# Reordering one-term matrix products against longer steps in two gated layers, and loading the first blocks in halves

## The chip, the cores and the metric

The kernel runs on one core of a Trainium2 chip, in float32. The metric is the device time of one execution in microseconds (us). A profile of one execution gives, for each engine, the instructions with their start and length.

## What is computed

The input x has 512 channels and 64 x 64 pixels. Four layers each add their result to x; each begins with a group normalization over 32 groups of 16 channels.

```python
x = x + attention(gn(x))         # layer 0: 8 heads, 4096 tokens, softmax over negative squared distances
x = x + gated_conv(gn(x), L1)    # layer 1
x = x + gated_conv(gn(x), L2)    # layer 2
x = x + linear_attention(gn(x))  # layer 3, with a 5 x 5 depthwise convolution

def gated_conv(x):               # both gated layers
    fused = conv1x1(x, w_in) + b_in          # 512 -> 1024 channels
    pwa, abc = fused[:128], fused[128:]
    dw0, dw1, dw2 = split(dwconv7(abc))      # 128, 256, 512 channels
    h = pwa * dw0
    h = (conv1x1(h, pw0) + pw0_b) * dw1
    h = (conv1x1(h, pw1) + pw1_b) * dw2
    return conv1x1(h, w_out) + b_out
```

## The kernel before

x stays on the chip as X: four chunks of 128 channels, each in eight blocks of 512 pixels. TensorE (PE) multiplies into PSUM banks of 128 x 512; VectorE (DVE) or ScalarE (ACT) evicts them. `matmul` (L1147) fixes TensorE's order to the order in which the Python code issues the steps; the order on DVE and ACT comes from the tile framework's scheduler, apart from instructions that are pinned.

**The beginning.** `load_x` (L171 to L174) issues X's chunks 0 and 1 block by block, chunk 0 on the SP queue and chunk 1 on the ACT queue; chunks 2 and 3 follow on SP (`load_later`). Each queue keeps at most four transfers in flight: a fifth is issued when the first has landed. `measure` (L623) computes the statistics of one block on DVE; `first` lists the 16 blocks of chunks 0 and 1, `rest` the 16 of chunks 2 and 3. `parameters` (L631) drives `_Norm.params`, a chain of small steps: aggregate, a small matmul, squares, a second matmul, `gn_a` (L136), a square root on ACT (L137), reciprocal (L139) and correction, `gains` (L638). At each of its two yields and once after the square root it calls a function `meanwhile`; here each call measures one block of `rest`. The gains scale the first weights (L426, L432), and the first matmul (`begin`) follows.

**The gated layers.** `_gated_convs` runs for L1 and L2. Three kinds of steps are written into lists:

- `inputs(i)`, called b12, b34 and b56: the first 1x1 convolution by a Strassen-like method of seven products (`_Seven.steps`), in groups of seven steps p1, p5, p7, p2, p6, p3, p4 for two chunks and two blocks. Each step multiplies two terms. p1, p5 and p7 open banks `ps[0]`, `ps[1]` and `ps[2]`; p2, p3 and p4 add their product to these same banks, and `put` then evicts them (ACT L1181 after p2, DVE L1188 and L1191 later). After p1 and p5 ACT copies the bank (`keep`, L1416); after p7 DVE adds the bank into `kept[1]` (L537).
- `blocks(gate, i)`, called g[i]: one step per block. A product of the earlier h with a pointwise weight, then one DVE instruction that adds the bias and multiplies by the convolved plane (L1489). g[1] and g[2] have one term, g[3] and later two.
- `outputs(3)`, `outputs(4)`: one-term products with the output weight, evicted by DVE into X (L1508, L1512).

These products share a pool of four PSUM banks (`ps_mm`); the convolution has four of its own (`ps_cv`).

`convolve(i, first, between)` runs the depthwise convolution of chunk i: first the steps of the list `first`, then bursts of 48 small matmuls (`ps_cv`, some 1.5 us each), with steps of `between` spread over the gaps; each step carries a weight (0.5 for a step of seven, 0.25 per term of the others) by which it is spread. After the last burst come the DVE transposes of the result (L1280, then four of 128 x 1024 at L1286), each followed by a bias on ACT (L1602), while the rest of `between` runs. g[i] needs the finished chunk i. During a convolution ACT also makes shifted copies (S, L1226) for the next one.

So around the end of `convolve(2)` TensorE's order is: last burst, g1[2..7], p1 and p5 of b56, g2[0..7], p7 and p2 of b56, first burst of `convolve(3)`. At the end of `convolve(5)` it is: last burst, out, out, out, then two gate products of two terms, first burst of `convolve(6)`.

Of the kernel before, what the change touches and what calls it, by code (L numbers as in the profile page):

```python
# [16 lines left out]
P = 128  # L17
# [4 lines left out]
BLK = 512  # L22
NB = N // BLK
# [123 lines left out]
def _all(pieces):  # L147
    for _ in pieces:
        pass
# [12 lines left out]
@with_exitstack  # L162
def trunk_kernel(ctx: ExitStack, tc: tile.TileContext, a: dict, out: bass.AP):
    nc = tc.nc

    base = ctx.enter_context(tc.tile_pool(name="base", bufs=1))
    small = ctx.enter_context(tc.tile_pool(name="small", bufs=1))


    X = base.tile([P, NC, N], FP, tag="X", name="X")  # L170
    def load_x(chunks, engines):  # L171
        for b in range(NB):
            for c, eng in zip(chunks, engines):
                eng.dma_start(out=X[:, c, ts(b, BLK)], in_=a["x"][c, :, ts(b, BLK)])  # L174

    load_x((0, 1), (nc.sync, nc.scalar))

    vec = base.tile([P, NVEC], FP, tag="vec", name="vec")

    def load_later():  # L180
        load_x((2, 3), (nc.sync, nc.sync))
        nc.sync.dma_start(out=vec, in_=a["vecs"])

    def vcol(name, i):
        at, n = _VEC_AT[name]
        return vec[:, at + i : at + i + 1]

    def vall(name):
        at, n = _VEC_AT[name]
        return vec[:, at : at + n]  # L190

    ident = base.tile([P, P], FP, tag="ident", name="ident")
    make_identity(nc, ident)

    gmask = base.tile([P, P], FP, tag="gmask", name="gmask")
    nc.gpsimd.memset(gmask, 1.0 / GROUP)
    for cm, step, first in ((1, -GROUP, 0), (-1, GROUP, GROUP - 1)):
        nc.gpsimd.affine_select(
            out=gmask,
            in_=gmask,  # L200
            compare_op=ALU.is_ge,
            fill=0.0,
            base=first,
            pattern=[[step, P // GROUP], [0, GROUP]],
            channel_multiplier=cm,
        )

    neg2 = base.tile([D, 1], FP, tag="neg2", name="neg2")
    nc.vector.memset(neg2, -2.0)

    def new_stats():
        return small.tile([P, NC, NB, 6], FP, tag="stats", name="stats")

    centered = _Centered(tc, small)

    dram = ctx.enter_context(tc.tile_pool(name="dram", bufs=1, space=bass.MemoryType.DRAM))
    F = [dram.tile([P, FORM.planes, FORM.plane], FP, tag=f"F{i}", name=f"F{i}") for i in range(NDW)]
    F3 = [
        dram.tile([P, FORM3.planes, FORM3.plane], FP, tag=f"G{i}", name=f"G{i}")
        for i in range(NQKV)  # L220
    ]
    Z = dram.tile([NB, BLK], FP, tag="Z", name="Z")
    R = dram.tile([32, 32], FP, tag="R", name="R")

    def others(stats, norm, *hint):

        stats, norm = _gated_convs(
            tc, a, X, vcol, vall, gmask, small, new_stats, centered, stats, norm, F
        )
        _linear_attention(  # L230
            tc, a, X, vcol, vall, ident, gmask, small, centered, stats, norm, F3, Z, out, *hint
        )

    def past():

        for eng in nc.engines:
            done = [i for i in nc.cur_bb.bb.instructions if i.engine == eng]
            with tc.issue_after(done[-1]):
                tc.mark_branch_hint_location("general", "LikelyTaken", engines=[eng])

    okay = small.tile([1, 1], mybir.dt.int32, tag="okay", name="okay")
    stats = new_stats()
    opool = tc.alloc_tile_pool(name="opool", bufs=1, side="right")
    O = [opool.tile([P, N], FP, tag=f"O{i}", name=f"O{i}") for i in range(NC)]
    norm = _attention_pairs(tc, a, X, O, gmask, small, centered, stats, okay, load_later, R)
    opool.release()
    others(stats, norm, past)

    found = nc.values_load(okay[0:1, 0:1])
    with tc.If(found < 1, label="general"):  # L250
        stats = new_stats()
        _attention(tc, a, X, ident, gmask, neg2, small, centered, stats)
        norm = _Norm(nc, small, gmask)
        centered.by(norm)
        with tc.tile_pool(name="ps_n", bufs=2, space=PSUM) as ps_n:
            _all(
                norm.params(0, NC - 1, stats, lambda: ps_n.tile([P, BLK], FP, tag="mm", name="gn_ps"))
            )
        for k in range(2):
            for c in range(NC - 1):  # L260
                centered.take(_pixels(FORM, X[:, c, :], k), c)
        others(stats, norm)
# [310 lines left out]
def _attention_pairs(tc, a, X, QO, gmask, small, centered, stats, okay, load_rest, R):  # L573
# [12 lines left out]
    nc = tc.nc  # L586
# [6 lines left out]
    with tc.tile_pool(name="att0", bufs=1) as p0, tc.tile_pool(  # L593
# [22 lines left out]
        def taken(b, c0, c1, engines=(None,)):  # L616
            for c in range(c0, c1):
                tc.keep_in_program_order(
                    centered.take(X[:, c, ts(b, BLK)], c, engines[c % len(engines)])
                )  # L620

        def measure(b, c):
            tc.keep_in_program_order(nc.vector.bn_stats(stats[:, c, b, :], X[:, c, ts(b, BLK)]))  # L623

        first = [(b, c) for b in range(NB) for c in range(2)]
        rest = [(b, 2 + c) for b, c in first]
# [5 lines left out]
        def parameters(c0, c1, meanwhile, known):  # L632

            norm.pause = meanwhile
            for _ in norm.params(c0, c1, stats, bank_gn, known):
                meanwhile()
            for n, g in enumerate((2 * scale * gain_in, gain_in)):
                nc.vector.tensor_scalar(gains[:, n, c0:c1], norm.r[:, c0:c1], g, None, ALU.mult)  # L638
# [10 lines left out]
        def scaled_first(n, eng, c0=0, c1=NC, pinned=False):  # L649
            centered.scaled(w_first[n], gains[:, n // 2 if n > 1 else n], eng, c0, c1, pinned)  # L650
# [5 lines left out]
            load_w(n, nc.sync)  # L656
        for at in first:
            measure(*at)
        parameters(
            0, 2, lambda: measure(*rest.pop(0)), lambda: taken(0, 0, 2, (None, nc.gpsimd))  # L660
        )
        scaled_first(2, nc.scalar, 0, 2, True)
        scaled_first(0, nc.gpsimd, 0, 2)
        for k in range(1, NB // 2):
# [657 lines left out]
def _gated_convs(ctx, tc, a, X, vcol, vall, gmask, small, new_stats, centered, stats, norm, F):  # L1322
# [4 lines left out]
    nc = tc.nc  # L1327
# [13 lines left out]
    for layer in ("L1", "L2"):  # L1341
# [28 lines left out]
        def taken(k, chunks=range(NC), eng=None):  # L1370
            for c in chunks:
                ins = centered.take(pc.pixels(X[:, c, :], k), c, eng)
                if pinned:
                    tc.keep_in_program_order(ins)
# [211 lines left out]
        def outputs(*chunks):  # L1586
            n = len(chunks) / 4
            return [
                (n, lambda b=b, o=o: output(chunks, b, o))
                for b in range(NB // 2, NB)  # L1590
                for o in range(NC if b == NB // 2 else NC - 1)
            ]
# [3 lines left out]
        def convolve(i, first, between):  # L1596


            D[i] = hp.tile([P, N], FP, tag="h", name=f"h{i}")

            def bias(t):
                nc.scalar.activation(t, t, AF.Identity, bias=vcol(pre + "dw_b", i))  # L1602

            taps = a[f"{layer}_T"]
            later = [] if i < 2 else None
            pc.ahead(i, 0, taps, later=later)
            for n, (_, f) in enumerate(first):
                f()
                if later and n == 3:
                    for _ in range(4):  # L1610
                        tc.keep_in_program_order(nc.scalar.copy(*later.pop(0)))
            for pair in later or ():
                nc.scalar.copy(*pair)

            parts = FORM.nr // FORM.run
            total = sum(n for n, _ in between)
            late = total / 12
            done = 0
            for part, _ in enumerate(pc.conv(i, 0, taps, bias, D[i], True)):
                upto = total - late * min(parts + 2 - part, 3)  # L1620
                if part < parts:
                    upto = upto * (part + 1) / parts
                while between and done + between[0][0] / 2 <= upto + 1e-6:
                    n, f = between.pop(0)
                    f()
                    done += n
            for _, f in between:
                f()

        b12, b34, b56 = (inputs(i) for i in (2, 4, 6))  # L1630
        g = [blocks(gate, i) for i in range(NDW)]
# [24 lines left out]
                f()  # L1656
        convolve(0, b12[:10], b12[10:])
        convolve(1, b34[:6], g[0] + b34[6:20])
        convolve(2, [], b34[20:] + g[1] + b56[:2])
        convolve(3, g[2] + b56[2:4], b56[4:16])  # L1660
        convolve(4, [], b56[16:] + g[3][:2])
        convolve(5, [(0, load_out)] + g[3][2:6], g[3][6:] + outputs(3) + g[4][:2])
        rest = outputs(4)
        convolve(6, [], g[4][2:] + rest[:9])

# [896 lines left out]
```

## Time and profile before

| | us |
|---|---|
| median of 3 runs (lowest, highest) | 3707.27 (3705.42, 3708.36) |
| the profiled execution | 3706.54 |
| its span | 3704.8 |
| first statistic on DVE starts | 4.62 |
| first matmul on X starts | 20.60 |
| L1: last burst of `convolve(2)` to first of `convolve(3)` | 2377.68 to 2400.84 |
| L2: the same | 2848.14 to 2871.61 |

The profile page lists busy time by engine, the chain of work that ended last, and the costliest groups of instructions. A weight load (PEld) goes ahead of each matmul record; a float32 product of 128 x 512 and one term makes two such records. In the timeline the bracket behind a row is the idle time before it and the instruction that ended it.

### The profile page before, as it was taken

What the parts mean: (1) busy time and instruction counts of PE and PEld (TensorE: products, weight loads), DVE (VectorE), ACT (ScalarE), POOL (GpSimd) and SP (SyncE); (2) the same over time, 40 slices, a digit from 0 to 9 for tenths busy, and PEclk for the clock granted to TensorE, in tenths of its full rate; (3) what the DMA queues carried; (4) which work ended last, traced back from release to release, by engine and by line L of the source; (5) the groups of instructions that cost most, each with busy time, mean ns of one, the idle gap of its engine ahead of it and who ended that gap; (6) DMA issues with size and microseconds to landing.
All of it is one profiled execution on the core that took longest, in us unless ns stands there. A gap on an engine that the chain in (4) does not pass through costs nothing.

```text
span 3704.8 us, 81755 instructions
## 1 busy us (share of the span) xinstructions
PE 3666.8 (99%) x35068; PEld 1695.2 (46%) x35068; DVE 2728.9 (74%) x3577; ACT 2061.9 (56%) x3007; POOL 228.8 (6%) x221
## 2 busy tenths in 40 slices
PE   7999999999999999999999999999999999999999
PEld 6544444444465443444433344554445544445543
DVE  6677777777765777877878868766778667776647
ACT  3577774777744777747575555673347632355210
POOL 1000000000000000010000000001100002232212
PEclk9999999999999999999999999999999999999999
DMA  2000000000000000000000015782157721575322
GB/s 103 10 7 7 4 7 12 4 7 7 7 4 10 7 4 7 7 12 4 4 7 4 7 53 169 199 222 63 34 154 202 214 73 51 159 195 125 84 59 95
DMA packets 186035, 222.77 MB, mean 60 GB/s; under 512 B 15800, under 2 KB 128696, under 8 KB 185536
## 3 DMA queue, kind: packets, MB, share of 16 engines
q1 hardware_dynamic: 160672, 156.26, 15.7%
q10 hardware_dynamic: 21312, 48.03, 3.6%
q0 software_dynamic: 3680, 13.18, 1.1%
q8 instruction: 277, 4.54, 0.5%
q14 instruction: 94, 0.77, 0.1%
HBM read 157.51 MB, written 59.90 MB: 59 GB/s over the span
## 4 chain that ended last, share of the span: by engine, by line
PE 92%; DVE 3%; DMA 2%; issue 1%; POOL 1%; ACT 0%; SPq 0%; ACTq 0%; DVEq 0%; POOLq 0%
PE ps L1147 25%; PE av L865 24%; PE ps_s L847 24%; PE ps L495 5%; PE ps_cv L1147 5%; PE vkp L1147 3%; PE ps L563 3%; PE ps_o L495 2%; PE ps_t L2058 1%; PE ps_o L926 1%; DMA S<-G 1%; DVE h L1286 0%; DVE h L1489 0%; POOL X L1569 0%; PE ps_M L1147 0%
## 5 line engine op out<-in xcount | busy, mean ns | idle before, releaser
L855 ACT ACTIVATE pt<-ps_s,A 128x512 f32<-128x512 f32 x2048 | 1284.3, 685 | 448.8 <-PE ps_s L847 438.6
L847 PE MATMUL ps_s<-O,K 64*64 64x512 f32 x8192 | 1417.4, 589 | 0.0
L1024 DVE TENSOR_TENSOR acc<-acc,pt 128x1024 f32<-128x1024 f32 x960 | 1177.1, 1226 | 325.1 <-ACT pt L855 298.8
L865 PE MATMUL av<-pt,O 64*64 64x512 f32 x4096 | 745.2, 589 | 0.0
L865 PE MATMUL av<-pt,V 64*64 64x512 f32 x4096 | 673.7, 589 | 0.0
L847 PEld LDWEIGHTS ps_s<-O,K 64*64 64x64 f32 x8192 | 436.3, 133 | 518.2 <-issue 468.1
L1226 ACT COPY S<-S 32x1295 f32<-32x1295 f32 (+1 forms) x256 | 321.3, 1256 | 158.7 <-DMA S<-F 70.2
L865 PEld LDWEIGHTS av<-pt,O 64*64 64x64 f32 x4096 | 236.3, 133 | 254.0 <-issue 241.3
L865 PEld LDWEIGHTS av<-pt,V 64*64 64x64 f32 x4096 | 209.4, 133 | 268.2 <-issue 253.8
L1147 PE MATMUL ps<-diff,w_sum 128*128 128x512 f32 x516 | 242.4, 600 | 1.4 <-DVE plane L1191 1.0
L1147 PEld LDWEIGHTS ps_cv<-S,T 64*32 64x32 f32 x13824 | 192.7, 105 | 110.8 <-issue 71.1
L1147 PE MATMUL ps_cv<-S,T 64*32 64x128 f32 x13824 | 232.7, 272 | 4.2 <-issue 3.0
L491 DVE TENSOR_TENSOR diff<-X,diff 128x512 f32<-128x512 f32 x200 | 134.4, 683 | 31.3 <-PE ps L1147 31.0
L491 DVE TENSOR_TENSOR diff<-X 128x512 f32<-128x512 f32 x200 | 132.2, 683 | 26.2 <-PE ps L495 14.2
L1147 PE MATMUL ps<-h,pw_L 128*128 128x512 f32 x320 | 147.9, 602 | 3.0 <-DVE h L1489 2.1
L1147 PE MATMUL ps<-h,w_out_L 128*128 128x512 f32 x320 | 147.8, 600 | 1.7 <-DVE X L1512 1.7
L1147 PEld LDWEIGHTS ps<-diff,w_sum 128*128 128x128 f32 x516 | 94.6, 190 | 117.9 <-issue 105.7
L1147 PE MATMUL ps<-X,w_in_L 128*128 128x512 f32 x304 | 143.9, 602 | 1.0 <-ACT w_in_L L426 0.8
L1280 DVE STREAM_TRANSPOSE h<-ps_cv 128x512 f32<-128x512 f32 x112 | 109.6, 1052 | 39.9 <-PE ps_cv L1147 39.5
L1147 PE MATMUL vkp<-kT,vT 128*128 128x512 f32 x256 | 115.2, 592 | 0.0
L537 DVE TENSOR_TENSOR kept<-kept,ps 128x512 f32<-128x512 f32 x73 | 49.9, 683 | 79.3 <-PE ps L495 28.2
L419 ACT ACTIVATE X<-X,gn_less 128x512 f32<-128x512 f32 x113 | 71.5, 709 | 52.6 <-DVE gn_less L129 52.6
(302 smaller groups left out, 3532.5 us busy)
## 6 DMA issues: line engine op xcount, KB each, us to landing
T<-in_L_T_dram SPq DMA_DIRECT2D x112, 384.0 KB, 4.5
F<-plane ACTq DMA_DIRECT2D x112, 324.0 KB, 3.7
S<-F SPq DMA_DIRECT2D x224, 162.0 KB, 4.8
S<-G SPq DMA_DIRECT2D x96, 153.0 KB, 4.3
row<-G SPq DMA_DIRECT2D x48, 272.0 KB, 3.6
T<-in_L_T_dram SPq DMA_DIRECT2D x48, 256.0 KB, 4.1
G<-plane POOLq DMA_DIRECT2D x33, 289.0 KB, 3.1
rd<-R SPq DMA_DIRECT2D x64, 128.0 KB, 2.9
```

Source lines behind the costliest of these rows:

```text
L419: return self.nc.scalar.activation(xs, xs, AF.Identity, bias=less)
L491: yield eng.tensor_tensor(t[j][c], a(c), b(c), ALU.subtract)
L495: self.matmul(ps, w[:, c], hs[c], start=(first and c == 0), stop=(c == 1), skip_group_check=not first,)
L537: nc.vector.tensor_add(kept[1], kept[1], ps[2])
L563: self.matmul(ps[:, ts(i, P)], hs[c][:, ts(i, P)], w[:, c], start=(first and i == c == 0), stop=(c == 1), skip_group_check=True,)
L847: nc.tensor.matmul(ps[ts(half, D), ts(h, BLK)], K[rows, t * P + half * D : t * P + (half + 1) * D], QO[pair][rows, cols], start=True, stop ...
L855: nc.scalar.activation(pt[:, ts(h, BLK)], ps[:, ts(h, BLK)], AF.Exp, bias=A[:, t, h : h + 1])
L865: nc.tensor.matmul(av[half][rows, :], v[keys, t * P + h * D : t * P + (h + 1) * D], pt[keys, ts(h, BLK)], start=(t == 0), stop=(t == NT - 1),)
L1024: nc.vector.tensor_add(acc, acc if u > 1 else first, pt)
L1147: self.tc.keep_in_program_order(self.nc.tensor.matmul(*args, **kw))
L1226: nc.scalar.copy(second, first)
L1280: nc.vector.transpose(out, src)
```

## The change

Three edits: the first block of chunks 0 and 1 is loaded as two halves of 64 partitions, one on each queue; of the three blocks of `rest` measured inside `parameters(0, 2, ...)` the third, after the square root, is measured later; and in `_gated_convs` the same steps are put into another order in the lists for `convolve(2)`, `convolve(3)` and `convolve(5)`.

```diff
+    def load_x(chunks, engines, b0=0):
+        for b in range(b0, NB):
...
-    load_x((0, 1), (nc.sync, nc.scalar))
+    for c in range(2):
+        for half, eng in enumerate((nc.sync, nc.scalar)):
+            rows = ts(half, P // 2)
+            eng.dma_start(out=X[rows, c, 0:BLK], in_=a["x"][c, rows, 0:BLK])
+    load_x((0, 1), (nc.sync, nc.scalar), 1)
...
-        parameters(
-            0, 2, lambda: measure(*rest.pop(0)), lambda: taken(0, 0, 2, (None, nc.gpsimd))
-        )
+        spare = [lambda: measure(*rest.pop(0))] * 2 + [lambda: None]
+        parameters(0, 2, lambda: spare.pop(0)(), lambda: taken(0, 0, 2, (None, nc.gpsimd)))
...
-        convolve(2, [], b34[20:] + g[1] + b56[:2])
-        convolve(3, g[2] + b56[2:4], b56[4:16])
+        mixed = g[1][:5] + b56[:1] + g[1][5:7] + b56[1:2] + g[1][7:]
+        convolve(2, [], b34[20:] + mixed)
+        convolve(3, g[2][:2] + b56[2:3] + g[2][2:5] + b56[3:4] + g[2][5:], b56[4:16])
         convolve(4, [], b56[16:] + g[3][:2])
-        convolve(5, [(0, load_out)] + g[3][2:6], g[3][6:] + outputs(3) + g[4][:2])
+        o3 = outputs(3)
+        mixed = g[3][6:7] + o3[:7] + g[3][7:] + o3[7:9] + g[4][:1] + o3[9:11] + g[4][1:2] + o3[11:]
+        convolve(5, [(0, load_out)] + g[3][2:6], mixed)
```

## The prediction

> **What bounds the kernel now.** I read the page first: the busy line and the chain that ended last.
>
> ```profile
> PE 3666.8 (99%) x35068; PEld 1695.2 (46%) x35068; DVE 2728.9 (74%) x3577; ACT 2061.9 (56%) x3007; POOL 228.8 (6%) x221
> PE 92%; DVE 3%; DMA 2%; issue 1%; POOL 1%; ACT 0%; SPq 0%; ACTq 0%; DVEq 0%; POOLq 0%
> ```
>
> TensorE is the bound nearly everywhere, so an edit pays only where TensorE waits. The waits view (its weight-load rows) says how much that is where the change works: 20.3 us in 38 waits for `gate`'s evictions at L1489, of which part is lead that a weight load has in any case.
>
> ```profile
> PEld ps L1147 <- DVE h L1489: 20.3, 38, 1.5
> ```
>
> Next the timeline of 2375 to 2400 us: the end of `convolve(2)` and the list that runs before `convolve(3)`, in layer L1.
>
> ```profile
> 2380.17 0.19 PEld L1147 LDWEIGHTS ps<-h,pw_L 128*128 128x128 f32 x1 [0.24 <-issue]
> 2380.60 0.19 PEld L1147 LDWEIGHTS ps<-h,pw_L 128*128 128x128 f32 x1 [0.24 <-issue]
> ...
> 2384.41 0.30 PEld L1147 LDWEIGHTS ps<-h,pw_L 128*128 128x128 f32 x2 [1.47 <-DVE h L1489]
> ...
> 2391.08 0.30 PEld L1147 LDWEIGHTS ps<-h,pw_L 128*128 128x128 f32 x2 [1.22 <-DVE h L1489]
> ...
> 2392.31 1.54 DVE L1489 SCALAR_TENSOR_TENSOR h<-ps,vec,h 128x512 f32<-128x512 f32 x2
> ...
> 2393.11 0.30 PEld L1147 LDWEIGHTS ps<-h,pw_L 128*128 128x128 f32 x2 [0.88 <-DVE h L1489]
> ...
> 2395.16 0.30 PEld L1147 LDWEIGHTS ps<-h,pw_L 128*128 128x128 f32 x2 [0.89 <-DVE h L1489]
> ...
> 2397.21 0.30 PEld L1147 LDWEIGHTS ps<-diff,w_sum 128*128 128x128 f32 x2 [0.89 <-DVE h L1489]
> ```
>
> Unhindered, loads follow each other by 0.43 us, and a product of one term is two of them: 0.86 us. From 2391.08 on the loads stand 2.03, 2.05 and 2.05 us apart where four would take 1.72: two products go out, TensorE waits until their evictions are over, two more go out. That pattern means two free PSUM banks, though `ps_mm` has four. The code says why: the seven-product step `p1` fills `ps[0]`, which stays taken until `p2` adds to it and `put` evicts it; `p5` holds `ps[1]` until `p3`, and `p7` holds `ps[2]` until `p4`. Before the change `p1` and `p5` (b56[:2]) stand ahead of the eight g[2] products, `p7` and `p2` (b56[2:4]) behind them.
>
> Last, the chain of waits of the first 70 us.
>
> ```profile
> 7.94 5.91 DMA X<-in_x_dram
> 13.86 0.02 issue
> 13.88 1.88 DVE stats L623 x3
> ...
> 18.23 0.16 DVE gn_a L136
> 18.38 0.60 DVE stats L623
> 18.98 0.08 DVE gn_r L139
> ```
>
> The landing of a late block of X, not the first, starts the last three statistics. And one statistic (0.60) stands between `gn_a` and the reciprocal.
>
> **The change, part by part.** No arithmetic is added or removed. The built order of each engine shows the moves: the same number of matmuls and of evictions, one more transfer on each of the SP and ACT queues.
>
> *Halved first blocks.* The first two 256 KB transfers become four of 128 KB. The first statistic now starts at 4.62; the first two landings are at about 4.6 and 4.77, two blocks sharing the engines, and later blocks land one per 0.67 us (19.35, 20.04, 20.72). So block c0 can land one block time, 0.65 us, earlier; c1's stays. But the third block's landing (5.89) and the wait at 13.86 follow from total bytes, and these are unchanged: the early start turns into a longer wait for the third block. Value 0. Bounds: if the queues ran in lockstep, the last block (14.61) would be taken at once, not at 15.08, a gain of 0.45; the extra issue on each queue (0.33 to 0.45 us) could cost 0.3. The ACT queue's two weight loads and the table load stand behind that issue; the table is needed at 18.42 and loaded by 10.6, which hides it.
>
> The Trainium skill ("DMA: Bandwidth & Descriptors", Issuing engines are not separate DMA queues) says transfers of both queues run on the same engines, and a second queue saves only issue time. By it this part is worth 0 as well; by the row's block time alone one would have booked 0.65.
>
> *One statistic less inside the parameters.* The square root runs 18.42 to 18.62; its second instance (32.16, reciprocal at 32.40) shows 0.03 us from its end to the reciprocal. So the reciprocal comes at 18.65, not 18.90: 0.25 us earlier, and gains, scaled weights and the first matmul (20.60) with it, since each follows the other without slack. The statistic (0.59) moves behind the gains, so the second pair of aggregates ends 0.34 later, at 28.66. TensorE asks for it 0.25 earlier, at 28.79. The cover of 0.72 us shrinks to 0.13; were it gone, the cost is 0.1. From 20.6 us on TensorE is busy and the waits view names no long one in the attention, so the start counts in full: -0.25, between -0.7 (with the lockstep) and +0.15 (with the issue and the lost cover).
>
> *g[1], g[2] and b56 mixed.* New TensorE order: g1[2..4], p1, g1[5..6], p5, g1[7], g2[0..1], p7, g2[2..4], p2, g2[5..7]. Between `p7` and `p2` three of the four banks are held. So g2[2], g2[3], g2[4] go through one bank: one product per round trip. The round trip is the row's 2.04 (0.53 to the second record, 0.59 until that one is done, 0.1 to DVE, 0.75 of eviction, 0.05 back). Per layer:
> - gone: the three waits of 2.04 - 1.72 = 0.32, together 0.96;
> - new: g2[3] and g2[4] each wait 2.04 - 0.86 = 1.18, together 2.36;
> - new: g2[6] needs the bank that `put` frees on ACT (L1181: 0.69 us, begun 0.04 after `p2`'s last record, which takes 0.59). That is 1.37 after this record's start, and g2[6] would go at 1.29: 0.1 of waiting and 0.1 of restart (0.53 between records in place of 0.43), 0.2;
> - kept: the waits of 0.81 and 0.56 that end at 2384.41 and 2391.08 (the matmul records before them start at 2383.17 and 2390.09; 0.43 off each gap). They pass to g1[7] and g2[1], which again meet bias transposes (L1286, 1.23 each, four of them) on DVE; two such transposes stand back to back in the new DVE order, so I add 0.15.
>
> 2.36 + 0.2 + 0.15 - 0.96 = +1.75 us per layer. L2 repeats the pattern (loads at 2861.85, 2863.89, 2865.94, 2867.98): +3.5 for both. Bounds per layer: +0.8 if the wait of 0.81 goes, because the step now between meets a freed bank, +2.6 if it doubles.
>
> Who else waits: the plane that L1181 writes leaves on the ACT queue about when it does now, so loads behind it do not move. DVE's backlog at the end is two evictions, about the 1.5 us of the convolution burst that follows.
>
> *g[3], outputs(3), g[4] mixed at the end of `convolve(5)`.* Here the stretch has no wait to remove: the windows view has TensorE busy for all of it, in both layers.
>
> ```profile
> 2503.00:2517.00 14.00, 14.00 (x286) 7.30 (x270) 11.58 (x15) 10.04 (x9) 0.00 (x0) 1.00 0.54 146
> 2975.00:2989.00 14.00, 14.00 (x310) 7.69 (x309) 12.37 (x15) 9.91 (x9) 0.00 (x0) 1.00 0.58 157
> ```
>
> New risk: the last group becomes gate, out, out, gate, out, out: six evictions in 6.9 us of TensorE. No bank is held here, so the fifth needs the first's bank, 5.2 us after the group starts. DVE has two transposes (0.9 each) and one of 1.15 first, then that eviction: done at 3.7. The sixth: done at 4.3, needed at 6.0. Value 0; if DVE came 2 us later, +0.5 per layer.
>
> **Sum.** -0.25 + 3.5 + 0 = +3.25 us. The profiled execution took 3706.54 (span 3704.8 and 1.7 around it): 3709.8 for it. The median of the runs shown is 3707.27, 0.7 above; I predict 3710.5.
>
> **Rivals.**
> *The mixing works as its name says.* In L1, 22 products stand between the bursts at 2379.21 and 2400.84: 21.63 - 22 x 0.858 - 0.24 for switching = 2.5 us of waiting; in L2 (2849.67 to 2871.61) 2.8. All gone, with the start: 3707.27 - 5.55 = 3701.7. For it: a two-term step gives DVE 1.72 us for one or no eviction. Against: the held banks. 0.16.
>
> *Slower: the clock falls in the new waits.* Place: g1[7] to g2[4], four waits of 0.6 to 1.2 us within 11 us. The trace has one price: from 20.60 to 24.18 matmuls come 0.85 apart, not 0.43, so 3.6 us at half rate lose 1.8. One such stretch per layer gives 3.25 + 3.6 = 6.9, 3714.1; to the end of the mixed stretch (some 11 us of products) 14, 3721. It decides beyond 0.2% from 4 us at half rate per layer. Against it: the present waits leave the clock at 1.00.
>
> ```profile
> 2377.00:2401.00 24.00, 22.78 (x154) 9.24 (x160) 22.28 (x33) 15.95 (x15) 0.00 (x0) 1.00 0.53 133
> ```
>
> The Trainium skill ("TensorE: Matmul & The Clock Gate", A second HAM failure mode) warns of just this: cycling through PSUM banks with micro-idles between groups made the clock swing. By it, this rival's 3714.1 or more; by the row just shown, nothing. I go by the row. 0.07.
>
> *Neutral*: kinder evictions and the ACT wait hidden, +1 or less, 3707.5: 0.09.
>
> **Numbers.** Forecast 0.68; by the bounds (-0.7 + 1.6 to 0.15 + 5.2 + 1) its own range is 3708.2 to 3713.6. The range 3704.5 to 3713.6 takes in the neutral case and the half of the first rival in which only some waits go. 0.2% is 7.4 us, about what a measurement of this kernel can tell from no change: faster by more would need more than all waits of both stretches (0.03); slower by more is the clock, or a doubled forecast (0.09); within, 0.88.
>
> **What would show it.** In the profile after: loads of g[2] 2.0 us apart with one product each, twice per layer; 23.2 us now from one burst's start (2377.68) to the next (2400.84), 24.9 then; no new wait at the end of `convolve(5)`; first matmul at about 20.35; first statistic near 4.0 with a longer wait for the third block. I am wrong if the stretch shortens, if the clock there is below 1.00, or if the first matmul moves by over 0.7.

## The result, and the profile after

The changed kernel takes 3713.44 us (median; 3709.21 to 3717.49), the kernel before on the same chip 3706.17 (3703.94 to 3708.57): ratio 1.0020, 95% interval 1.0013 to 1.0027, +7.3 us. Forecast: 3710.5, in 3704.5 to 3713.6; as a difference, +3.25. The profiled execution took 3713.56 with a span of 3711.8, 7.0 more than before.

The page's busy line and chain look as before, so where the 7 us lie has to come from the stages.

```profile
PE 3667.0 (99%) x35068; PEld 1699.9 (46%) x35068; DVE 2728.8 (74%) x3577; ACT 2061.9 (56%) x3007; POOL 230.0 (6%) x221
PE 91%; DVE 3%; DMA 2%; issue 2%; ACT 1%; POOL 1%; SPq 0%; ACTq 0%; DVEq 0%; POOLq 0%
```

| starts at (us; last row: length) | before | after | added since the row above |
|---|---|---|---|
| first matmul on X | 20.60 | 22.58 | 1.98 |
| first score matmul of the attention | 123.53 | 126.72 | 1.22 |
| first burst, `convolve(0)` of L1 | 2255.66 | 2258.86 | 0.00 |
| last product with the output weight, L2 | 3129.75 | 3137.05 | 4.10 |
| span | 3704.8 | 3711.8 | -0.28 |

Of the 4.10, the stretches between the bursts of `convolve(2)` and `convolve(3)` give 1.63 in L1 (23.16 to 24.79) and 1.78 in L2 (23.47 to 25.25). The other 0.7 are mostly waits without a releaser inside bursts, which differ from profile to profile.

**The mixed stretch.** The timeline of L1 around the g[2] products (start, length, engine, operation; in brackets the idle time before it and its releaser):

```profile
2393.78 0.50 PEld L1150 LDWEIGHTS ps<-diff,w_sum 128*128 128x128 f32 x2 [0.36 <-DVE h L1492]
...
2395.38 0.19 PEld L1150 LDWEIGHTS ps<-h,pw_L 128*128 128x128 f32 x1 [0.24 <-issue]
...
2396.87 0.75 DVE L1492 SCALAR_TENSOR_TENSOR h<-ps,vec,h 128x512 f32<-128x512 f32 x1
2397.67 0.30 PEld L1150 LDWEIGHTS ps<-h,pw_L 128*128 128x128 f32 x2 [1.67 <-DVE h L1492]
...
2398.84 0.75 DVE L1492 SCALAR_TENSOR_TENSOR h<-ps,vec,h 128x512 f32<-128x512 f32 x1 [0.62 <-PE ps L1150]
2399.64 0.30 PEld L1150 LDWEIGHTS ps<-h,pw_L 128*128 128x128 f32 x2 [1.67 <-DVE h L1492]
...
2403.27 0.30 PEld L1150 LDWEIGHTS ps<-h,pw_L 128*128 128x128 f32 x2 [0.75 <-ACT plane L1184]
```

p7 starts at 2393.78; g[2][2], [3] and [4] load at 2395.38, 2397.67 and 2399.64: one product per round trip, TensorE waiting for DVE and DVE for TensorE. At 2403.27 stands the forecast short wait for L1184 (L1181 before).

**The beginning.** The chain of waits of the first 30 us:

```profile
0.80 2.85 DMA X<-in_x_dram
3.67 7.51 DMA X<-in_x_dram
11.19 5.46 DMA X<-in_x_dram
16.65 0.02 issue
16.68 1.29 DVE stats L627 x2
...
20.43 0.17 DVE gn_a L136
...
20.86 0.18 DVE gn_r L139
...
22.58 0.79 PE ps L567 x2
```

The last block of X lands at 16.65 and DVE takes it at once; before, the last block landed at 14.61. The transfer view of 2 to 30 us, 40 slices of 0.7 us, before and then after (first row: busy tenths of the DMA engines):

```profile
DMA  5899999999999999999999999999999999991000
GB/s 99 275 369 372 413 398 404 416 386 401 372 383 398 366 389 395 383 389 392 386 386 383 389 386 389 383 386 386 392 389 386 380 389 364 357 324 73 6 0 0
```

```profile
DMA  4997899999999999999998999999999999999982
GB/s 123 351 222 123 249 304 296 319 328 334 378 413 392 404 389 383 334 383 351 386 348 287 369 378 357 337 369 395 392 357 392 369 401 410 378 383 390 364 317 102
```

From 3.4 to 9 us the engines are 70% busy or more and move 123 to 334 GB/s instead of 369 to 416. The number of bytes is the same; the rate is not.

### The profile page after: what moved, and what is told of

It reads as the page before. It is cut to its first block, busy times and chain, and to the rows that moved or that the text cites. A ratio compares the mean times of both kernels' runs of the same rounds, so it can differ in the third digit from the quotient of the medians.

```text
span 3711.8 us, 81750 instructions
## 1 busy us (share of the span) xinstructions
PE 3667.0 (99%) x35068; PEld 1699.9 (46%) x35068; DVE 2728.8 (74%) x3577; ACT 2061.9 (56%) x3007; POOL 230.0 (6%) x221
## 4 chain that ended last, share of the span: by engine, by line
PE 91%; DVE 3%; DMA 2%; issue 2%; ACT 1%; POOL 1%; SPq 0%; ACTq 0%; DVEq 0%; POOLq 0%
PE ps L1150 24%; PE av L868 24%; PE ps_s L850 24%; PE ps L499 5%; PE ps_cv L1150 5%; PE vkp L1150 3%; PE ps L567 3%; PE ps_o L499 2%; PE ps_t L2064 1%; PE ps_o L929 1%; DVE h L1289 0%; DMA X<-in_x_dram 0%; POOL X L1572 0%; DMA S<-F 0%; ACT S L1229 0%
## 5 line engine op out<-in xcount | busy, mean ns | idle before, releaser
L1492 DVE SCALAR_TENSOR_TENSOR h<-ps,vec,h 128x512 f32<-128x512 f32 x96 | 70.5, 743 | 46.8 <-PE ps L1150 46.0
```

The source lines that it names most:

```text
L1492: nc.vector.scalar_tensor_tensor(d, ps, bias, d, ALU.add, ALU.mult)
```

## The experiments

Each is the kernel before with one edit. First the whole change split in two, and two other orders.

```diff
 halves: the halved first blocks alone
 mix23: the new lists of convolve(2) and convolve(3) alone
 mix3: the new list of convolve(3) alone
 closed:
+        convolve(2, [], b34[20:] + g[1] + b56[:7])
+        convolve(3, g[2], b56[7:16])
```

**halves.** 

> The kernel before with the halved first blocks alone (queues and everything else as before). Theory A, the halves themselves delay the data: in the profile of the changed kernel the stretch in which the first blocks land moved 123 to 250 GB/s where before it moved 370 to 410, with the DMA engines as busy, the second statistic started at 6.82 instead of 5.23 and the 16th at 17.29 instead of 15.08. Then this kernel shows the same hole: second statistic at 6.5 or later, first matmul on X at 22.3 to 23.2 (20.60 + 2.0 + the 0.22 of the reciprocal that it does not have), first score matmul 3 to 4 later than 123.53, time 3 to 4 us above before. Rival B, a disturbance of that one execution: second statistic near 4.8 to 5.3, first matmul at 20.2 to 20.7, time within 1 us of before. Rival C, the loss comes from the statistic that was dropped from the parameters: as B here, and seen in the kernel with that edit alone.

**mix23.** 

> The kernel before with the new order for convolve(2) and convolve(3) alone. Theory H, held banks (p1, p5 and p7 hold three of four banks, so three gate products go through one): the stretch between the bursts is 24.8 in L1 and 25.2 in L2 as in the changed kernel (23.16 and 23.47 before), the beginning is that of before, time 3 to 4 us above before. Rival, the longer stretch comes from something that the later start or the convolve(5) edit carried into it (other transfers, other phase): stretch near 23.3, time within 1 us of before.

**mix3.** 

> Of the new orders only that of convolve(3): p1 and p5 stand ahead of g[2] as before, p7 after g[2][1] and p2 after g[2][4]. Theory H (one free bank between p7 and p2): loads of g[2][2] to g[2][4] stand about 2.0 apart with one product each, two new waits of 1.0 each, the three waits of 0.2 to 0.3 at g[2] gone; stretch +1.0 to +1.6 per layer over 23.16 and 23.47. Rival D (DVE is the limit in this stretch, 22.3 of 24 us busy, so waits only change places): the sum of waits stays within 0.4 of before, 2.9 in L1 and 3.3 in L2.

**closed.** 

> Another order: the whole group of seven (p1 to p4 of b56[:7]) stands between g[1] and g[2], so that no bank is held while g[2] runs: convolve(2) gets b34[20:] + g[1] + b56[:7], convolve(3) gets g[2] ahead and b56[7:16] between. Theory H: the three waits of 0.2 to 0.3 at g[2] go, and of the waits of 0.81 and 0.56 at least the second, since seven two-term steps give DVE 12 us with little to evict: 1.5 to 2.5 us less waiting per layer, time 3 to 5 us below before. Rival D: DVE has the same work and the waits come back elsewhere (g[1] or the next burst): within 1 us of before.

Then a paced form of closed, the halves cut otherwise, and the statistic alone.

```diff
 closed_paced:
+        convolve(2, [], b34[20:] + g[1] + b56[:7])
+        convolve(3, g[2], b56[7:19])
+        convolve(4, [], b56[19:] + g[3][:5])
+        convolve(5, [(0, load_out)] + g[3][5:6], g[3][6:] + outputs(3) + g[4][:2])
 own_queue: for half in range(2): for c, eng in enumerate((nc.sync, nc.scalar)): ...
 column_halves: X[:, c, ts(half, BLK // 2)], half 0 on SP, half 1 on ACT
 measure_later: the spare list of the change alone
```

**closed_paced.** 

> As closed, but convolve(3) keeps its 12 steps between the bursts: convolve(2) gets b34[20:] + g[1] + b56[:7], convolve(3) gets g[2] ahead and b56[7:19] between, convolve(4) b56[19:] + g[3][:5], convolve(5) load_out and g[3][5:6] ahead. In closed the waits for gate's evictions were gone (4.25 us in the kernel before, none there), but TensorE stood still for 2.24 us before the fifth burst of convolve(3), at 2420.2 and again in L2, and the granted clock was 0.57 in the 4 us after it. Theory P (nine steps between the bursts instead of twelve let the bursts overtake the copies S that ACT makes, 1.27 us each): both stops go, the waits for gate stay away, so 3 to 4 us less waiting than in the kernel before. Rival Q (ACT is late because p1, p5 and p2 of the group take its time, wherever the bursts stand): a stop of 2 us remains near the fifth burst, and the time is that of closed. Rival R (the three steps taken from convolve(4) starve its own bursts): a stop in convolve(4).

**own_queue.** 

> Halved first blocks as in the run halves, but both halves of a chunk on that chunk's own queue (chunk 0 on SP, chunk 1 on ACT). There are as many transfers, of the same size and shape. Theory E (a transfer of 64 partitions moves slowly, or its extra issue holds the queue up): the hole is there as in halves, second block's statistic late, 16th statistic at 16.3 or later, first matmul on X at 22.3 or later. Rival F (the hole needs both queues at work on one block's two halves): no hole, 16th statistic at 14.6 to 15.1, first matmul at 20.3 to 20.9.

**column_halves.** 

> The first blocks halved by columns instead of partitions: each of the four transfers covers 128 partitions and 256 pixels, the halves on both queues as in the run halves. Theory E1 (64 partitions are what is slow): no hole, 389 GB/s or so from 4 us on as in before, 16th statistic near 15, first matmul at 20.3 to 20.9. Rival E2 (more and smaller transfers, the extra issue, or fewer bytes in flight): the hole stays, first matmul at 22 or later.

**measure_later.** 

> The kernel before with the dropped statistic alone. By the prediction's step the reciprocal follows the square root at once: from gn_a to the first matmul 2.15 instead of 2.37, first matmul on X at 20.3 to 20.6, second pair of aggregates in time (TensorE does not wait for it), first score matmul 0.2 earlier than 123.0 to 123.5. Rival: the later aggregates hold TensorE up by 0.2 to 0.6 us, and the first score matmul comes no earlier.

Last, with edits as their texts say:

**paced_and_measure.** 

> closed_paced together with the dropped statistic, whole first blocks: the parts that the runs showed to gain. Expected from their rows: no wait for gate's evictions (4.25 us in the kernel before), 0.23 less from gn_a to the first matmul on X, so some 1 to 4 us below before, 3704 to 3707 on this chip's scale of 3708 for before. Rival: other waits of TensorE without a releaser in the trace (0.5 to 1.3 us each in the bursts, 3.5 to 5.7 us in all) differ by chance by as much, and the two kernels cannot be told apart.

**second_halved.** 

> The first blocks whole, the second blocks of chunks 0 and 1 halved by partitions over both queues instead. Theory G (halved blocks open the hole wherever they stand: shorter transfers leave the two queues out of step with each other): first two statistics as before at 4.6 and 5.2, then a hole after the second blocks, 16th statistic at 16.0 or later where whole blocks gave 14.6 to 15.1. Rival K (only the first transfers, at the cold start, are sensitive): 16th statistic at 14.6 to 15.1.

**vec_first.** 

> All blocks whole, but the 54 KB load of vec moved from the end of the SP queue to its front, so that chunk 0's blocks start one small transfer later than chunk 1's. Theory S (what counts is that both queues' blocks start together): packets longer than 0.3 us appear between 3 and 9 us as in the halved kernels, 16th statistic at 16 or later. Rival H (halving itself): the 54 KB cost 0.14 us at 390 GB/s and an issue of 0.45, 16th statistic at 14.8 to 15.4.

**mix2.** 

> Of the new orders only that of convolve(2): p1 after g[1][4], p5 after g[1][6]; p7 and p2 stay behind all of g[2], so at most two banks are held while gate products run. Theory H (held banks): no wait of 1.0 between single products; two by two with waits of 0.2 to 0.3 at g[2] as before, the early waits of 0.8 and 0.6 somewhere else; sum of waits for gate's evictions within 0.5 us of 2.1 per layer, stretch 23.0 to 23.7. Rival: the mixed order delays gate's evictions by itself, stretch 24.5 or longer.

### What the beginning showed

| kernel (starts in us, one profile each) | 2nd, 16th statistic on DVE | gn_a to first matmul on X | first matmul on X |
|---|---|---|---|
| before | 5.23, 15.08 | 2.37 | 20.60 |
| seven others with whole blocks, untouched queues | 5.07 to 5.27, 14.62 to 14.95 | 2.37 to 2.38; 2.14, 2.15 without the statistic | 19.98 to 20.48 |
| after | 6.82, 17.29 | 2.15 | 22.58 |
| halves | 5.54, 16.63 | 2.38 | 22.16 |
| own_queue | 6.02, 16.62 | 2.37 | 22.14 |
| column_halves | 4.77, 17.12 | 2.37 | 22.64 |
| second_halved | 5.43, 16.52 | 2.38 | 22.04 |
| vec_first | 6.44, 16.07 | 2.37 | 21.59 |

Eight profiles with whole blocks have the 16th statistic at 14.62 to 15.08, five with halved blocks at 16.52 to 17.29: 2.05 between the means (14.79, 16.84). So A holds against B and C, with a smaller effect than it expected in halves: the second statistic came at 5.54 and not at 6.5 or later, and the time rose by 1.8 us and not by 3 to 4. One queue per chunk doesn't mend it (F falls), nor do 128 partitions (E1 falls); column_halves has issues of 0.38 to 0.45 as before, so the longer issues of half transfers (0.57 to 0.86) aren't the cause either. With the second blocks halved, the hole comes after them (217 GB/s in the fifth and sixth slice), so G holds against K:

```profile
GB/s 91 295 410 325 217 217 325 351 337 319 351 377 322 398 410 413 395 407 386 386 386 386 389 378 395 380 386 386 401 375 378 378 395 375 392 353 373 239 53 6
```

vec_first, with all blocks whole, lies between: 1.3 us lost, most of it before 5 us, where H had booked 0.14 for the bytes and 0.45 for the issue. Its 16.07 misses H's 14.8 to 15.4 and just meets S's mark of 16, so a small transfer ahead of whole blocks does part of the same. A rival that E2 names is fewer bytes in flight: with halves among a queue's four transfers, three blocks are under way instead of four. In after it doesn't hold: by the trace's issues and packets 1.52 MB were issued and not yet moved at 4.8 us, 1.29 in before, and the next 0.7 us moved 249 GB/s against 413. For second_halved (0.76 MB there) it stays open. From 3.4 to 9 us after has 25 packets of 0.3 to 1.3 us among those of 0.084, before has one; why they take that long stays open.

The statistic is worth 0.23, as booked: 2.14 and 2.15 in place of 2.37. The rival's hold-up isn't seen: in measure_later no wait for a gain or weight stands between 21 and 41 us. But its first score matmul came no earlier (124.08), because the slow start of TensorE, with matmuls 0.85 apart, lasted 6.0 us. Over the fourteen profiles this stretch is 3.2 to 6.2 us long (before 3.6, after 6.2); after's 1.22 us between first matmul and attention is this, half of 2.5.

What sets the length can be read from the trace's records of the granted clock. They begin where the fast matmuls begin, at 24.24 us in before and 28.75 in after; for the time ahead of that the windows view has no record and prints 1.00. The times between two changes of the clock are whole multiples of 3.413 us in every trace (the 3679.57 us of before are 1078 of them), so each trace can be cut into windows of 3.41 us. In all fourteen profiles the slow stretch ends with the first window that TensorE fills (3.25 us busy or more); one with 2.76 was not enough. Two windows of after (length; PE, PEld, DVE, ACT, POOL busy; clock, DMA share, GB/s):

```profile
21.92:25.33 3.41, 2.75 (x7) 1.72 (x8) 3.41 (x8) 2.53 (x5) 3.23 (x3) 1.00 1.05 380
25.33:28.75 3.42, 3.42 (x15) 2.90 (x15) 3.42 (x7) 0.58 (x1) 2.00 (x2) 1.00 1.07 386
```

In after the first matmul falls 0.66 us into a window and TensorE has to fill the next one too; in before it falls 0.22 ahead of a window's start. The windows lie differently in each profile (they are shifted by 0.08 to 3.23 us against the span's start), so the length is a matter of chance and not of an edit; how much of the 1.22 stands in the medians no run shows. The Trainium skill ("TensorE: Matmul & The Clock Gate", What's actually happening) has the clock decided over a free-running window of about 3.4 us, so that the end of the slow stretch depends on where in the window the first matmul falls. The records agree with that, while the half microsecond either way that the section allows is too little for a spread of 2.9.

### What the lists showed

| kernel | L1, L2 stretch | first burst to last output product |
|---|---|---|
| before | 23.16, 23.47 | 874.1 |
| six others in the old order | 22.95 to 23.40, 22.74 to 23.47 | 873.2 to 875.8 |
| after | 24.79, 25.25 | 878.2 |
| mix23 | 25.11, 25.27 | 877.4 |
| mix3 | 24.61, 25.93 | 880.8 |
| mix2 | 23.25, 23.42 | 874.1 |
| closed, closed_paced | other steps between | 881.3, 873.5 |

mix23 repeats the longer stretch without the late start. mix3 has it too (+1.45 in L1, inside the expected 1.0 to 1.6, and +2.46 in L2), mix2 has not: what costs is p7 and p2 among the g[2] products. The waits view of 2370 to 2430 us (who waited for whom: us, times, longest) for before, after and mix3, two rows each:

```profile
PE ps L1147 <- DVE h L1489: 1.0, 2, 0.6
DVE h L1489 <- PE ps L1147: 0.5, 1, 0.5
```

```profile
DVE h L1492 <- PE ps L1150: 4.1, 5, 1.8
PE ps L1150 <- DVE h L1492: 2.9, 4, 0.8
```

```profile
DVE h L1489 <- PE ps L1147: 4.1, 5, 1.8
PE ps L1147 <- DVE h L1489: 2.7, 4, 0.9
```

D falls on the rows of DVE's waits: they rise from 0.5 to 4.1 us while TensorE's rise from 1.0 to 2.9 and 2.7, so it isn't DVE's load but the single bank that both hand back and forth. In L2 of mix3 the clock fell after the second such wait; the timeline there:

```profile
2868.57 0.30 PEld L1147 LDWEIGHTS ps<-h,pw_L 128*128 128x128 f32 x2 [1.71 <-DVE h L1489]
2870.54 0.36 PEld L1147 LDWEIGHTS ps<-h,pw_L 128*128 128x128 f32 x2 [1.67 <-DVE h L1489]
2871.41 0.34 PEld L1147 LDWEIGHTS ps<-X,w_in_L 128*128 128x128 f32 x1 [0.51 <-issue]
2872.26 0.34 PEld L1147 LDWEIGHTS ps<-X,w_in_L 128*128 128x128 f32 x1 [0.52 <-issue]
```

and the windows view:

```profile
2870.00:2874.50 4.50, 3.96 (x6) 1.66 (x7) 1.24 (x2) 0.64 (x1) 0.00 (x0) 0.62 0.00 0
```

Loads of one step stand 0.85 apart and the clock is 0.62: this stretch is 1.3 longer than L1's. It is one of six layers with these waits (two each in after, mix23 and mix3); in the other five the clock stayed at 1.00 here.

closed removes TensorE's waits for gate's evictions, and loses more: at the fifth burst of `convolve(3)`,

```profile
2412.00:2420.00 8.00, 5.94 (x246) 3.96 (x231) 4.43 (x6) 7.08 (x7) 0.00 (x0) 1.00 0.80 210
2420.00:2424.00 4.00, 3.79 (x17) 1.39 (x16) 0.00 (x0) 1.75 (x2) 0.00 (x0) 0.57 0.55 149
```

TensorE stands still for 2.24 us, ACT is busy for 7.08 of 8 with copies S, and the clock falls to 0.57. In L2 a like stop of 2.11 us ends at 2896.1 and leaves the clock at 1.00, so the length of a stop alone doesn't decide it. closed takes 3713.68 to 3709.99 of before, ratio 1.0008 (0.9999 to 1.0017).

What decides can be read from the same windows of 3.41 us. In all fourteen traces the clock changes only at the end of one; inside a run it falls to 0.50 and for one window. Here are closed's fall, the window ahead of it and the one with most of the stop in L2, then mix3's window ahead of its fall and the one with most idle time in its L1:

```profile
2420.13:2423.54 3.41, 3.33 (x17) 1.39 (x16) 0.00 (x0) 1.62 (x2) 0.00 (x0) 0.50 0.58 163
2416.72:2420.13 3.41, 1.25 (x83) 1.02 (x75) 1.97 (x2) 2.60 (x3) 0.00 (x0) 1.00 0.77 202
2894.58:2898.00 3.42, 1.88 (x51) 1.20 (x51) 0.58 (x1) 2.19 (x3) 0.00 (x0) 1.00 0.74 208
2867.32:2870.73 3.41, 1.69 (x4) 0.49 (x4) 2.55 (x4) 3.27 (x3) 0.00 (x0) 1.00 0.00 0
2392.87:2396.28 3.41, 2.07 (x5) 0.41 (x3) 2.79 (x5) 3.34 (x4) 0.00 (x0) 1.00 0.00 0
```

The stop in L1 lies in one window and leaves 1.25 us of TensorE's work in it; the stop in L2 is shared by two, which keep 2.84 and 1.88. Only mix3's L2 has both waits of a pair in one window (1.69 busy); the other five pairs leave 2.07 or more in each. Over the fourteen traces, windows with up to 1.66 us idle were never followed by a fall, and those with 1.72 or more always were, but for two within the last 8 us of a run (1.75 and 2.01 idle). So about half a window of idle time is what cost the clock here; PE's busy times are partly modelled, so the bound is rough. halves and mix23 each lose a window at 3308 and 3307 us, in layer 3, which neither edits: single profiles differ by 1.7 us through this alone.

closed_paced, with twelve steps between the bursts, keeps the clock at 1.00 there:

```profile
2412.00:2420.00 8.00, 7.30 (x164) 3.97 (x146) 4.29 (x6) 6.23 (x6) 0.00 (x0) 1.00 0.71 181
2420.00:2424.00 4.00, 4.00 (x103) 2.07 (x101) 1.98 (x3) 3.41 (x4) 0.00 (x0) 1.00 0.68 198
```

Its eight g[2] products run without a wait, so P holds against Q; a stop of 0.70 is left at 2416.4 in L1, and there is one of 1.13 in the last burst of `convolve(4)` (R, if it is that: the trace names no releaser for either). Of the 4.25 us of waits that its expectation counts, the time from first burst to last output product got back 0.6, which lies within the 873.2 to 875.8 of the old order; with the same lists, paced_and_measure took 874.5. Part of the waiting came back elsewhere, as closed's rival D said: TensorE's waits for L1191, over the whole run in before and in closed_paced:

```profile
PE ps L1147 <- DVE plane L1191: 1.0, 2, 0.5
PE ps L1147 <- DVE plane L1191: 2.7, 4, 1.0
```

Times: closed_paced 3706.37 to 3708.18, paced_and_measure 3708.10 to 3709.98, both with ratio 0.9996 (0.9987 to 1.0005): not told apart from before, as the rival of paced_and_measure said. halves (3711.76) and mix23 (3713.21) against 3709.99 gave 1.0008 each (0.9998 and 0.9999 to 1.0017); their excesses add up to 1.0016, the whole change's 1.0020 within the intervals, but each interval alone still holds 1: the split rests on the traces.

## Why the prediction was right, and where it failed

- **Held banks** (+3.5): right in mechanism and size. 1.63 and 1.78 measured for 1.75 a layer; the two new waits added 1.11 each (1.18 booked), the three old ones went, and the early ones stayed (0.81 and 0.56 became 0.86 and 0.62, all in L1). The skill's rule on cycling through banks asked for a clock below 1.00; in the changed kernel the row decided, 1.00 in both layers. mix3's 1.3 us in L2 show that the rival exists all the same; it priced the fall from the slow start and had no row on when it comes.
- **Reciprocal** (-0.25): right, 0.23.
- **Halves** (0, from the sentence that the third block's landing and the wait at 13.86 "follow from total bytes"): this is the step that failed. It took the rate of before, one block per 0.67 us, as given, and the runs show 2.05 us lost to a lower rate. Its bounds (0.45 gained, 0.3 lost) were made from issue times and landings alone; no row of before showed a half transfer, and nothing excluded a lower rate. The skill's rule (no more engines behind a second queue) gave 0 too; no run speaks against it, but it doesn't bear on this loss.
- **The start as a whole** (-0.25) came to +3.2: 2.0 by data and reciprocal together, 1.2 by the slow start of TensorE, which was not in the sum and whose length varies by 2.9 us without any edit (1.4 us of time).
- **`convolve(5)`** (0): right in that TensorE stands idle there for no eviction of a gate or output product. The stage took 0.2 us longer in L1 and 0.8 in L2 (32.1 to 32.9); 0.5 and 0.73 are stops inside a burst without a releaser, and the old order gives 31.9 to 33.2 in L2.
- **Signs of being wrong**: the first matmul moved by 2.0, more than the 0.7 set as the limit. So the number lay in the range while the term for the halves was wrong by 2.
- **Luck in the number**: the difference, +7.3, is more than twice the forecast +3.25 and above its own bounds (0.9 to 6.35). The time is within 0.2 us of the range's end, and inside it also because the kernel before ran at 3706.17 in this comparison, 1.1 less than the 3707.27 that the forecast was added to.

## What to carry to other kernels

An order is judged by how many buffers it holds open at each step: putting long steps among short ones helps only if the long ones don't keep the buffers that the short ones turn over. Work between bursts also paces the copies that the bursts need; moving three steps of it forward left closed's bursts waiting. Splitting a transfer leaves the bytes alone but not the rate, so a price of zero "by bytes" needs an upper bound from a measured split.

## What the runs showed of the hardware

Halving two of sixteen transfers, in any of four ways, cut the rate from about 390 GB/s to between 123 and 351 for some 5 us with the DMA engines mostly 60% busy or more; in column_halves a second such stretch followed, to 16 us. The granted clock changed only on a grid of 3.41 us: it fell to 0.50 for one window after windows in which TensorE stood idle for 1.72 us or more (two at the ends of runs excepted), and of two like stops of 2.1 to 2.2 us only the one inside a single window cost it. TensorE's slow first stretch, 3.2 to 6.2 us in kernels with the same beginning, lasted until TensorE had filled a window.
